# Softplus in a Mamba block: its three parts added by TensorE in PSUM in place of two VectorE additions

## The chip, the cores and the metric

The kernel runs on one core of one Trainium2 chip. The metric is the device time of one execution in microseconds (us). The engines are TensorE (PE, with its weight loads PEld), VectorE (DVE), ScalarE (ACT) and GpSimd (POOL); SyncE (SP) issues most of the DMAs.

## The reference

The program is a hybrid network of two layers on 32 sequences of 256 tokens with 128 features: a bidirectional Mamba block, a recurrence, two attention blocks and several mixtures of experts. Only the Mamba block is touched by the change. For each of two directions (the sequence as it is, and reversed) it computes:

```python
xz = x @ in_w.T;  xc, z = split(xz)                  # 256 inner features each
xc = silu(causal_conv(xc) + conv_b)
dt, Bm, Cm = split(xc @ xp_w.T)                      # 8, 16 and 16 columns
delta = softplus(dt @ dtp_w.T + dtp_b)
h = exp(delta * A) * h + (delta * u) * B             # 16 states per inner feature
y = sum(h * C) + xc * D
y = (y * silu(z)) @ out_w.T
```

The change is in how `softplus` is put together. The kernel has no softplus function to call; it uses softplus(v) = max(v, 0) + ln(1 + d) with d = exp(-|v|). Since 1 + d is rounded in 32 bits, it also adds what the rounding lost, d - ((1 + d) - 1). So delta is a sum of three parts: the logarithm, the correction, and max(v, 0).

## The kernel before

**Units.** `unit(k)` is a generator that does one direction of one chunk of 512 tokens (two sequences): a forward unit ("f") and then a backward unit ("b") for each of 16 chunks, 32 units in all. Features lie on the 128 partitions, the two halves of the 256 inner features side by side, so most tiles of the preparation are 128 x 1024 in 32-bit floats. `pipeline(unit, 16, 32)` (line 641) starts a new unit every 16 rounds and advances every active unit by one `yield` a round, the oldest first. A unit prepares for 24 rounds and then scans for 16, so that the preparation of one unit lies beside the scans of the unit before it.

**Preparation.** In the order of the text: the convolution as matmuls (lines 470 and 477), Silu (`act`, line 482), the projection to dt, B and C (488 and 490), written to DRAM (492). The softplus: a matmul gives v in PSUM (498), ScalarE computes `du` = max(v, 0) (499), |v| (500), `delta` = d (501), `one` = 1 + d (505) and `lg` = ln(one) (506). VectorE then makes the negated correction in place in `one` (508), subtracts it from `lg` (509), and adds `du` (510), which gives `delta`. GpSimd multiplies `delta` and `act` into `du` (511). Both go to DRAM (518) and come back in the layout of the scans (`load`, 545). The gate is a matmul of its own (521) and a Silu on ScalarE (530). ScalarE switches its function tables between Silu, Ln and Exp: each switch is an ACT_TABLE_LOAD of its own in the profile.

**Scans.** A unit has 8 groups of 4 scans. For each scan ScalarE computes `dA` (line 602, Exp, into one of three PSUM tiles), GpSimd `dBu` (606, four buffers), and VectorE scans (615). The products with C are made by VectorE (617 for two scans at once into `pr2`, two buffers; 625 for a third) and GpSimd (563, the fourth), and TensorE sums them over the states into `yps` (568) one group later.

**PSUM.** `pair()` gives the tile `m` of two banks, with one buffer: every matmul result of the preparation passes through this tile in turn, and the next one waits until the last reader of the one before is done.

**Order.** The engines execute their queues in order. The framework that records the kernel places the instructions into these queues by its own estimate of when each can start, so that the order on an engine is not just that of the text. `behind_scans()` ties a few VectorE instructions to the scan before them.

The lines that the change and the prediction speak of stand in this code:

Of the kernel before, what the change touches and what calls it, by code (L numbers as in the profile page):

```python
# [17 lines left out]
AF = mybir.ActivationFunctionType  # L18
ALU = mybir.AluOpType
# [3 lines left out]
P = 128  # L23
# [53 lines left out]
def halves(v):  # L77

    v = np.asarray(v)
    return np.moveaxis(v.reshape(2, P, *v.shape[1:]), 0, 1)  # L80


def col(v):
    return np.asarray(v).reshape(-1, 1)


def spaced(w, x):

    w = np.asarray(w)
    out = np.zeros((w.shape[0], 8, 16), np.float32)  # L90
    out[:, :, :HD] = w.reshape(w.shape[0], 2, 8, HD)[:, x]
    return out.reshape(w.shape[0], P)


def pack_inputs(i):
    mam, com, att, row, taps = (Packed() for _ in range(5))
    turn = np.arange(DI).reshape(2, 32, 4).transpose(0, 2, 1).reshape(DI)

    p = "L0_attn_a_"
    for s in "fb":  # L100

        w = i[p + "in_w_" + s]
        mam.add("in_w" + s, np.concatenate([w[:DI], w[DI:][turn]]).T)


        xp = i[p + "xp_w_" + s]
        turned = [xp[at : at + DS].reshape(4, 4, DI).transpose(1, 0, 2).reshape(DS, DI) for at in (DTR, DTR + DS)]
        mam.add("xp" + s, halves(np.concatenate([xp[:DTR], *turned, np.zeros((1, DI), np.float32)]).T))
        mam.add("out" + s, i[p + "out_w_" + s][:, turn])
        dtp = np.zeros((DTR + 2 * DS + 1, DI), np.float32)  # L110
        dtp[:DTR], dtp[-1] = i[p + "dtp_w_" + s].T, i[p + "dtp_b_" + s]
        mam.add("dtp" + s, dtp)
        mam.add("conv_b" + s, i[p + "conv_b_" + s].reshape(1, -1))

        a = np.asarray(i[p + "A_log_" + s]).reshape(2, 32, 4, 4, 4)
        mam.add("A_log" + s, a.transpose(1, 4, 0, 3, 2).reshape(P, 32))
        mam.add("D" + s, halves(i[p + "D_" + s]))
        taps.add(s, i[p + "conv_w_" + s][:, 0, :].T.reshape(1, -1))
    mam.add("one_row", np.eye(DTR + 2 * DS + 1, dtype=np.float32)[:, -1:])
    mam.add("turn", np.eye(P, dtype=np.float32)[:, turn[:P]])  # L120
    mam.add("proj", halves(i[p + "proj_w"].T))
    mam.add("proj_b", col(i[p + "proj_b"]))
    mam.add("g", col(i[p + "ln_gamma"]))
    mam.add("b", col(i[p + "ln_beta"]))

    p = "L0_ffn_"
    com.add("pw", i[p + "pw_w"].T)
    com.add("dw", i[p + "dw_kernel"][:, 0, :])
    com.add("dw_b", col(i[p + "dw_bias"]))
    com.add("pw_b", col(i[p + "pw_b"]))  # L130
    com.add("rt0", i[p + "router_w"].T)
    com.add("exp_w", i[p + "expert_w"].transpose(2, 0, 1))
    com.add("exp_b", i[p + "expert_b"].T)
    com.add("f0_out", i[p + "out_w"].T)
    com.add("f0_out_b", col(i[p + "out_b"]))
    com.add("norm_w", col(i[p + "norm_w"]))
    com.add("ffd", i[p + "ff_down_w"].T)
    com.add("ffd_b", col(i[p + "ff_down_b"]))
    com.add("ffu", i[p + "ff_up_w"].T)
    com.add("ffu_b", col(i[p + "ff_up_b"]))  # L140
    row.add("rt0_b", i[p + "router_b"].reshape(1, -1))

    p = "L0_attn_b_"
    for n in "ABC":
        com.add("rnn" + n, i[p + n].T)
    com.add("rnn_g", col(i[p + "gamma"]))
    com.add("rnn_b", col(i[p + "beta"]))

    p = "L1_attn_a_"
    for n, part in (("q", 0), ("k", 1)):  # L150
        w = i[p + "qkv_w"][:, part * P : (part + 1) * P]
        b = i[p + "qkv_b"][part * P : (part + 1) * P].reshape(1, P)
        for x in range(2):
            att.add(f"a{n}{x}", spaced(w, x))
            att.add(f"ab{n}{x}", spaced(b, x).T)
    att.add("wv", i[p + "qkv_w"][:, 2 * P :])
    row.add("bv", i[p + "qkv_b"][2 * P :].reshape(1, -1))
    att.add("rq", i[p + "rq_w"])
    att.add("rq_b", col(i[p + "rq_b"]))
    att.add("rkv", i[p + "rkv_w"])  # L160
    att.add("rk_b", col(i[p + "rkv_b"][:32]))
    row.add("rv_b", i[p + "rkv_b"][32:].reshape(1, -1))
    att.add("rout", i[p + "rout_w"])
    att.add("rout_b", col(i[p + "rout_b"]))
    att.add("aout", i[p + "out_w"])
    att.add("aout_b", col(i[p + "out_b"]))
    for n in ("gl", "gr"):

        g = np.zeros((H, HD, H, HD), np.float32)
        for h in range(H):  # L170
            g[h, :, h, :] = i[p + n + "_w"]
        att.add(n, g.reshape(P, P))

    p = "L1_attn_b_"
    swap = np.arange(P) ^ 1
    for n in ("Wq", "Wk"):
        for x in range(2):
            att.add(f"{n}{x}", spaced(i[p + n].T, x))
            att.add(f"{n}s{x}", spaced(i[p + n][swap].T, x))
    att.add("Wv", i[p + "Wv"].T)  # L180
    att.add("Wo", i[p + "Wo"].T)

    p = "L1_ffn_"
    att.add("f1_g", col(i[p + "ln_gamma"]))
    att.add("f1_b", col(i[p + "ln_beta"]))
    att.add("rt1", i[p + "router_w"])
    att.add("sgu", i[p + "shared_gate_up_w"])
    att.add("sdn", i[p + "shared_down_w"])
    gu = np.ascontiguousarray(i[p + "gate_up_w"])
    dn = np.ascontiguousarray(i[p + "down_w"].reshape(E, FF // P, P, P).transpose(0, 2, 1, 3))  # L190

    return mam, com, att, row, taps, gu, dn
# [81 lines left out]
def hybrid_kernel(ctx: ExitStack, tc, x_d, out_d, d, packs):  # L274
    nc = tc.nc
    mam, com, att, row, tap, cst, cst1 = (packs[k] for k in ("mam", "com", "att", "row", "tap", "cst", "cst1"))
# [13 lines left out]
    def K(name):  # L290
        return cst.view(cst_t, name) if name in cst.at else cst1.view(late_t["cst1"], name)
# [8 lines left out]
    ident = K("ident")  # L300
# [51 lines left out]
    with ExitStack() as ph:  # L352
# [4 lines left out]
        def M(name):  # L357
            return mam.view(mam_t, name)

        wconv, wout, A, skip = {}, {}, {}, {}  # L360
        with tc.tile_pool(name="mtap", bufs=1) as tp, tc.tile_pool(name="mprep", bufs=2, space=PSUM) as pp:
            tap_t = tp.tile([P, tap.n], F32, name="tap_t")
            nc.scalar.dma_start(tap_t, d["tap"].partition_broadcast(P))
            for k, s in enumerate("fb"):

                wconv[s] = wp.tile([P, DCONV, DI], F32, name="wconv" + s)
                at, _, w = tap.at[s]
# [45 lines left out]
        def unit(k):  # L413
# [3 lines left out]
            def pair():  # L417
                return ps.tile([P, 2, CH], F32, tag="m", name="m", bufs=1)

            def both(tag, bufs):  # L420
                return p2.tile([P, 2, CH], F32, tag=tag, name=tag, bufs=bufs)

            if s == "f":
                m = pair()
# [8 lines left out]
                m = pair()  # L433
# [11 lines left out]
                m = pair()  # L445
# [20 lines left out]
            m = pair()  # L466
            for h in range(2):
                for j in range(DCONV):
# [5 lines left out]
                        start=(j == 0),  # L474
                        stop=False,
# [10 lines left out]
            m = pair()  # L486
# [8 lines left out]
            delta, du = both("delta", 1), both("du", 1)  # L495
            m = pair()
# [5 lines left out]
            yield  # L502

            one, lg = both("sp", 1), both("lg", 1)
            nc.scalar.activation(one, delta, AF.Identity, bias=1.0)
            nc.scalar.activation(lg, one, AF.Ln)
            yield
            nc.vector.scalar_tensor_tensor(one, one, -1.0, delta, ALU.add, ALU.subtract)
            nc.vector.tensor_sub(lg, lg, one)
            nc.vector.tensor_add(delta, lg, du)  # L510
            nc.gpsimd.tensor_mul(du, delta, act)
            yield

# [5 lines left out]
            m = pair()  # L519
            for h in range(2):  # L520
# [4 lines left out]
                    start=True,  # L525
                    stop=True,
# [5 lines left out]
            for n, at in (("B", 0), ("C", DS)):  # L532
# [1 line left out]
                nc.sync.dma_start(  # L534
                    bc[n].rearrange("p g t -> p (g t)"), rows_of(xdbl_d, at, ((0, 32), (4, 4)), 4)
                )
            for _ in range(5):
                yield


# [93 lines left out]
            if s == "b":  # L634
                m = pair()
# [3 lines left out]
                yield  # L639

        pipeline(unit, 16, 2 * NCH)

    late = ctx.enter_context(tc.tile_pool(name="late", bufs=1))
# [15 lines left out]
    n = SPARE // 30  # L659
# [1050 lines left out]
```

## Time and profile before

| what | value |
|---|---|
| median of 3 runs | 6272.99 us (6271.46 to 6285.75) |
| the profiled execution | 6280.36 us, of which its span 6278.6 us |
| TensorE busy over the span | 5317.6 us (85%) |
| VectorE busy | 4184.9 us (67%) |
| ScalarE busy | 2664.6 us (42%) |
| GpSimd busy | 3335.2 us (53%) |
| end of the Mamba stage (last line 638) | 2104 us |

The profile shows one execution. Its slices divide the span into 40 equal parts of 157 us and give the busy tenths of each engine; the Mamba stage is slices 1 to 13 and part of 14. Queries of the trace give the busy times of a stretch, the waits of an engine ("A <- B" is A waiting for B), and the instructions in order of time: start in us, duration in us, engine, line, operation, output <- inputs, shapes, and in brackets the idle time before it and what ended it. A matmul of 32-bit floats appears as two records.

### The profile page before, as it was taken

The page shows a single profiled execution, that of the slowest core. Times are in us where ns is not written, and L with a number is a line of the kernel's source. Part 1 is how long each engine was busy: PE and PEld are TensorE (multiplying, and loading weights), DVE is VectorE, ACT ScalarE, POOL GpSimd, SP SyncE. Part 2 cuts the span into 40 slices and gives each one's busy share as a digit, 9 for nine tenths or more (in the row PEclk, how much of TensorE's full clock was granted, in tenths as well). Part 3 has the DMA queues.
Part 4 walks back from the last instruction along what each step waited for, and adds up shares of the span by engine and source line. Part 5 has one row for each costly group of instructions (what it writes and reads, how often), then busy time and mean ns, then how long its engine had stood idle before and what let it go on. Part 6 is the DMA issues. An engine that isn't in the chain of part 4 may idle for free. (4 is left out here: it accounts for less than half of the span.)

```text
span 6278.6 us, 73286 instructions
## 1 busy us (share of the span) xinstructions
PE 5317.6 (85%) x25538; PEld 2731.4 (44%) x25538; DVE 4184.9 (67%) x7070; ACT 2664.6 (42%) x4376; POOL 3335.2 (53%) x3074
## 2 busy tenths in 40 slices
PE   6777777777776799999989889897998999998897
PEld 2111111111111366865534444445884444444786
DVE  5999999999999664044645555554665666664565
ACT  4565555556565355334524434432221333333221
POOL 5888888888888565034634444443332333333332
PEclk8887888888888899588989999998998999997998
DMA  3232233322332660000000000003550000000555
GB/s 153 115 122 115 108 129 121 116 108 112 119 122 114 235 257 1 1 1 1 1 1 8 9 10 8 8 11 104 188 188 22 18 18 18 18 11 11 188 187 187
DMA packets 190417, 512.08 MB, mean 82 GB/s; under 512 B 22176, under 2 KB 75168, under 8 KB 164960
## 3 DMA queue, kind: packets, MB, share of 16 engines
q1 hardware_dynamic: 172192, 468.00, 20.7%
q0 software_dynamic: 17280, 35.69, 1.7%
q8 instruction: 202, 3.31, 0.2%
q10 hardware_dynamic: 576, 3.71, 0.2%
q14 instruction: 167, 1.37, 0.1%
HBM read 359.93 MB, written 147.38 MB: 81 GB/s over the span
## 5 line engine op out<-in xcount | busy, mean ns | idle before, releaser
L606 POOL TENSOR_TENSOR dBu<-widedu,bcB 128x512 f32<-128x512 f32 x1024 | 1334.0, 1324 | 250.7 <-DVE h L615 132.8
L615 DVE TENSOR_TENSOR_SCAN h<-dA,dBu 128x512 f32<-128x512 f32 x768 | 941.3, 1226 | 108.7 <-ACT dA L602 37.8
L568 PE MATMUL yps<-pr,cst_t 128*32 128x512 f32 x2048 | 702.5, 719 | 300.0 <-POOL pr L563 129.4
L930 POOL TENSOR_SCALAR_AFFINE_SELECT e<-e 128x2048 f32<-128x2048 f32 (+1 forms) x256 | 343.1, 1352 | 600.7 <-ACT e L1041 388.5
L1406 POOL DMA_INDIRECT rows_out<-y,goes x284 | 271.8, 957 | 558.5 <-DVE y L1404 451.5
L602 ACT ACTIVATE dA<-widedelta,Af 128x510 f32<-128x510 f32 x512 | 351.3, 689 | 398.4 <-DVE h L615 311.0
L994 DVE TENSOR_REDUCE nm<-st 128x2 f32<-128x512 f32 x512 | 324.3, 684 | 267.6 <-PE st L990 266.7
L602 ACT ACTIVATE dA<-widedelta,Ab 128x510 f32<-128x510 f32 x512 | 346.9, 687 | 354.5 <-DVE h L615 237.1
L568 PEld LDWEIGHTS yps<-pr,cst_t 128*32 128x32 f32 x2048 | 98.8, 120 | 870.2 <-POOL pr L563 308.1
L1181 ACT ACTIVATE s<-s 128x512 f32<-128x512 f32 x284 | 179.0, 630 | 575.9 <-DVE s L1180 329.2
L314 POOL TENSOR_TENSOR rstd<-var,cst_t 128x4 f32<-128x4 f32 x128 | 130.0, 1016 | 514.0 <-DVE var L312 512.1
L775 POOL TENSOR_TENSOR comb<-comb,ye 128x512 f32<-128x512 f32 x224 | 284.7, 1275 | 181.2 <-DVE ye L774 74.8
L1054 ACT ACTIVATE e<-st 128x512 f32<-128x512 f32 x512 | 271.6, 599 | 178.0 <-PE st L1050 146.0
L563 POOL TENSOR_TENSOR pr<-hs,bcC 128x512 f32<-128x512 f32 x256 | 339.8, 1328 | 13.3 <-DVE hs L615 13.0
L615 DVE TENSOR_TENSOR_SCAN hs<-dA,dBu 128x512 f32<-128x512 f32 x256 | 308.9, 1207 | 16.5 <-ACT dA L602 16.5
L1295 POOL DMA_INDIRECT rows_in<-xt,slot x256 | 254.0, 992 | 119.5 <-issue 99.1
L617 DVE TENSOR_TENSOR pr<-h,bcC 128x1024 f32<-128x1024 f32 x256 | 309.9, 1210 | 7.8
L1182 DVE TENSOR_TENSOR hh<-s,u_ps 128x512 f32<-128x512 f32 x284 | 195.3, 688 | 169.8 <-ACT s L1181 165.5
L1387 PE MATMUL g_ps<-xb,gu 128*128 128x256 f32 x1136 | 302.1, 389 | 3.6 <-ACT xb L1370 2.3
L1396 PE MATMUL yps<-dn,hh 128*128 128x128 f32 x2272 | 290.6, 276 | 5.3 <-DVE hh L1182 5.3
L1387 PE MATMUL u_ps<-xb,gu 128*128 128x256 f32 x1136 | 293.4, 381 | 0.0
L1396 PEld LDWEIGHTS yps<-dn,hh 128*128 128x128 f32 x2272 | 282.4, 192 | 14.0 <-DVE hh L1182 6.8
(348 smaller groups left out, 11021.0 us busy)
## 6 DMA issues: line engine op xcount, KB each, us to landing
gu<-in_gu SPq DMA_DIRECT2D x142, 512.0 KB, 3.7
rows_in<-zero SPq DMA_DIRECT2D x60, 1170.0 KB, 18.7
widedelta<-delta_d SPq DMA_DIRECT2D x64, 1024.0 KB, 6.8
widedu<-du_d SPq DMA_DIRECT2D x64, 1024.0 KB, 5.1
dn<-in_dn SPq DMA_DIRECT2D x142, 256.0 KB, 3.9
bcB<-xdbl_d SPq DMA_DIRECT2D x32, 1024.0 KB, 5.3
bcC<-xdbl_d SPq DMA_DIRECT2D x32, 1024.0 KB, 7.2
xr<-rows_in SPq DMA_DIRECT2D x142, 130.0 KB, 3.9
```

The costliest lines, as they stand in the source:

```text
L563: nc.gpsimd.tensor_mul(pr, hs, bc["C"][:, g, :])
L568: nc.tensor.matmul(yps[32 * k : 32 * k + 32, :], K("states"), pr, start=False, stop=(g == 3), skip_group_check=True, tile_position=(0, 32 ...
L602: nc.scalar.activation(two(dA)[:, :, 1:L], two(steps)[:, :, 1:L], AF.Exp, scale=A[s][:, at : at + 1])
L606: nc.gpsimd.tensor_mul(dBu, duw[:, k, :], bc["B"][:, g, :])
L615: scan[0] = nc.vector.tensor_tensor_scan(*views, 0.0, ALU.mult, ALU.add)
L617: nc.vector.tensor_mul(pr2, h2, bc["C"][:, g, :].unsqueeze(1).to_broadcast([P, 2, CH]))
L775: nc.gpsimd.tensor_add(comb, comb, ye)
L930: nc.gpsimd.affine_select(e, e, [[0, n], [sign, P]], ALU.is_gt, 0.0, base=base, channel_multiplier=-sign)
L994: nc.vector.tensor_reduce(n1[:, x, 2 * r : 2 * r + 2], o.rearrange("p (j k) -> p j k", j=2), AX.X, ALU.max, negate=True,)
L1387: nc.tensor.matmul(o[:, j, :], gu[:, at : at + P], xb, start=True, stop=True)
L1396: nc.tensor.matmul(yps[:, t, :], hh[:, k, t * P : (t + 1) * P], dn[:, k, :], start=(k == 0), stop=(k == FF // P - 1),)
L1406: i = nc.gpsimd.indirect_dma_start(rows_out[:, :], bass.IndirectOffsetOnAxis(ap=goes[:, t : t + 1], axis=0), y[:, t, :], None)
```

## The change

In the changed kernel `one` holds -(1 + d) (the bias comes from a new column `minus` of -1 in the packed weights), and Ln takes it with scale -1. One VectorE instruction makes the correction with its own sign. Then six matmuls through the identity (three inputs for each of the two halves) add `lg`, `one` and `du` in a tile `m` in PSUM, and ScalarE copies the sum into `delta`. GpSimd's product follows as before. The softplus has one round more; one round of the later waiting is taken out, so that the loads and the scans stay in the same rounds. Lines of the changed kernel after the softplus are six higher than before (509, the VectorE instruction; 515, the matmuls; 516, the copy; 517, the product).

```diff
+    mam.add("minus", np.full((P, 1), -1.0))
...
             one, lg = both("sp", 1), both("lg", 1)
-            nc.scalar.activation(one, delta, AF.Identity, bias=1.0)
-            nc.scalar.activation(lg, one, AF.Ln)
-            yield
-            nc.vector.scalar_tensor_tensor(one, one, -1.0, delta, ALU.add, ALU.subtract)
-            nc.vector.tensor_sub(lg, lg, one)
-            nc.vector.tensor_add(delta, lg, du)
+            nc.scalar.activation(one, delta, AF.Identity, bias=M("minus"), scale=-1.0)
+            nc.scalar.activation(lg, one, AF.Ln, scale=-1.0)
+            yield
+            nc.vector.scalar_tensor_tensor(one, one, 1.0, delta, ALU.add, ALU.add)
+            yield
+
+            m = pair()
+            for h in range(2):
+                for n, t in enumerate((lg, one, du)):
+                    nc.tensor.matmul(m[:, h, :], ident, t[:, h, :], start=(n == 0), stop=(n == 2))
+            nc.scalar.copy(delta, m)
             nc.gpsimd.tensor_mul(du, delta, act)
             yield
...
-            for _ in range(5):
+            for _ in range(4):
                 yield
```

## The prediction

> **What bounds the kernel now.** I read the slices of the span first, then the busy time of the Mamba stage alone, then who waits for whom in it, then the queues instruction by instruction around two softplus blocks. (The chain that ended last covers only the expert layers at the end, and no line of this change.) Row of the slices, and busy times of a stretch of 30 whole units (columns: length, PE, PEld, DVE, ACT, POOL, granted clock, DMA share, GB/s):
>
> ```profile
> DVE  5999999999999664044645555554665666664565
> ...
> 100.00:2050.00 1950.00, 1390.28 (x3435) 357.32 (x3434) 1793.24 (x1704) 1128.21 (x1432) 1702.03 (x1291) 0.83 0.30 117
> ```
>
> The Mamba stage ends at 2104 us with line 638. In it VectorE is busy in 92% of the time and GpSimd in 87%, TensorE in 71%, ScalarE in 58%. What VectorE waits for in the same stretch:
>
> ```profile
> DVE h L615 <- ACT dA L602: 37.8, 45, 2.7
> DVE sp L508 <- ACT lg L506: 23.1, 15, 1.6
> DVE hs L615 <- ACT dA L602: 16.5, 15, 1.4
> ```
>
> That is 77.4 us, all on ScalarE (columns: us in total, times, longest); TensorE and GpSimd are not in the list, and GpSimd's own waits are on VectorE. So VectorE sets the stage; its instructions otherwise start back to back. The order of both kernels as built, put side by side, is the same on every engine after the Mamba stage, and all tiles lie at the same addresses. So the whole effect lies in those 2104 us.
>
> Now the two softplus blocks of one pair of units. First on VectorE, the forward unit's (from 923 us) and the backward unit's (from 980 us):
>
> ```profile
> 923.27 1.39 DVE L508 SCALAR_TENSOR_TENSOR sp<-sp,delta 128x1024 f32<-128x1024 f32 x1 [1.56 <-ACT lg L506]
> 925.33 1.23 DVE L615 TENSOR_TENSOR_SCAN h<-dA,dBu 128x512 f32<-128x512 f32 x1 [0.66 <-ACT dA L602]
> 926.47 1.21 DVE L509 TENSOR_TENSOR lg<-lg,sp 128x1024 f32<-128x1024 f32 x1
> 927.59 1.22 DVE L615 TENSOR_TENSOR_SCAN h<-dA,dBu 128x512 f32<-128x512 f32 x1
> 928.72 1.21 DVE L510 TENSOR_TENSOR delta<-lg,du 128x1024 f32<-128x1024 f32 x1
> 929.84 1.21 DVE L617 TENSOR_TENSOR pr<-h,bcC 128x1024 f32<-128x1024 f32 x1
> ...
> 980.27 1.68 DVE L509 TENSOR_TENSOR lg<-lg,sp 128x1024 f32<-128x1024 f32 x1
> 981.88 1.22 DVE L615 TENSOR_TENSOR_SCAN h<-dA,dBu 128x512 f32<-128x512 f32 x1
> 983.02 1.20 DVE L510 TENSOR_TENSOR delta<-lg,du 128x1024 f32<-128x1024 f32 x1
> 984.14 1.21 DVE L615 TENSOR_TENSOR_SCAN h<-dA,dBu 128x512 f32<-128x512 f32 x1
> ```
>
> An operation costs VectorE the distance to the next start, not its duration. ScalarE at the first of these blocks:
>
> ```profile
> 917.49 1.05 ACT L505 ACTIVATE sp<-delta 128x1024 f32<-128x1024 f32 x1
> 918.55 1.28 ACT L530 ACT_TABLE_LOAD   x1
> 919.85 1.02 ACT L530 ACTIVATE gate<-m 128x1024 f32<-128x1024 f32 x1
> 920.89 1.28 ACT L506 ACT_TABLE_LOAD   x1
> 922.18 1.06 ACT L506 ACTIVATE lg<-sp 128x1024 f32<-128x1024 f32 x1
> 923.26 1.28 ACT L602 ACT_TABLE_LOAD   x1
> 924.55 2.73 ACT L602 ACTIVATE dA<-widedelta,Ab 128x510 f32<-128x510 f32 x4
> ```
>
> In the forward unit the gate's Silu stands ahead of Ln, so VectorE waits 1.56 us for Ln and 0.66 us for the next dA.
>
> **Removed from VectorE.** Lines 509 and 510. Forward unit: 927.59 - 926.47 = 1.12 and 929.84 - 928.72 = 1.12. Backward: 1.61 and 1.12. A pair of units: 4.97 us. Unit 0 has no scans beside it and is counted below; the other 31 units are 15.5 pairs: **77 us** off the engine that sets the stage. The kept line 508 has the same two inputs and I leave its price.
>
> **Added on TensorE.** Six matmuls through the identity a unit. The nearest row has the same shape and type:
>
> ```profile
> 973.60 1.99 PE L521 MATMUL m<-xpad,mam_t 128*128 128x512 f32 x4 [0.82 <-DVE x L638]
> ```
>
> Two matmuls (four records) take 1.99 us, so six take 6.0; over 30 units 179, and TensorE rises from 1390 us to some 1570 of about 1865 (84%). I cost this at nothing. What covers it: products of a group of four scans reach TensorE a group later, and prod2 has two buffers, prod four (two a group), so VectorE needs a group's buffers back only two groups on. A group lasts 7.0 us (L615 starts at 862.79 and 869.80). The convolution already puts 10.1 us of matmuls in that queue (925.48 to 935.57), and no wait of VectorE on TensorE follows. The six split: one waits for Ln alone, five (5.0 us) for line 509 of the new kernel. Queued behind them are one group's L568 products (lines 574 now). Cover gone, the price is up to 6.0 us a unit.
>
> **Added and moved on ScalarE.** A copy of 128x1024 out of PSUM a unit. Row: line 499, the same shape out of PSUM, 1.02 us. As built, the gate now follows the copy in every unit, since both use the one PSUM pair m; so it no longer shares a table switch with Ln in the forward units. Exp reloads rise from 78 to 94: 16 x 1.28 = 21 us. ScalarE grows by 53 us to some 1180 of 1865 (63%). What counts is whether dA comes late.
>
> Gain: in the forward unit Ln starts 2.3 us earlier (gate and its table gone from ahead of it) less one dA moved in front of it (0.69). Walked on from 917.49: dA to 919.2, table, Ln to 921.6, table, next dA at 923.5. VectorE, free at 921.7, does one scan to 922.9, line 509 to 924.2, the next scan at once. The 1.56 and the 0.66 are gone: 2.2 us a pair.
>
> Loss: copy, two dA, then table, Silu, table: 3.6 us without a dA, 4.3 until the next is ready. Three dA tiles let ScalarE run three scans ahead, at 7.0/4 = 1.75 us a scan 5.2 us of cover, 3.6 where the three have no product between them. In the forward unit the five matmuls end at 929.2, the copy's turn comes at 929.8, and the dA after the gate is ready at 937.1, scan needed at 937.7: no wait. In the backward unit POOL's product releases TensorE at about 981.7, the sum is there at 986.7, two microseconds after the copy's turn, and the dA after the gate is about 0.9 us late. I take 1.0 us a pair; bounds 0 and 5.6 (2.8 in each unit: copy 1.0 plus 4.3 less a cover of 3.6, plus a wait of 1.1 for the sum). The rest of the 77.4 I leave as it is. Net over 15 pairs: (2.2 - 1.0) x 15 = **18 us gained**; between 51 lost and, if every wait went, 77 gained.
>
> The Trainium skill speaks against the extra switches: "ScalarE: Activation LUTs", section "What ACT_TABLE_LOAD costs", gives 1283 ns and a drain of about 1380 ns for every switch. Here the load starts 0.01 us after the operation before it ends, and Silu 0.02 after the load: no drain shows, 1.28 is the price. By the page 16 switches would take 43 us of ScalarE and the gate's stretch 6.4 us, past the cover by about 1.9: 16 x 1.9 = 30 us lost, and a gain of 63 in place of 93. I take the row.
>
> **Moved on GpSimd and the queues.** The product du (line 517, 2.35 us) waits for the copy; queued behind it are dBu products, for which scans wait. It now stands after dBu 17 and 53 of a pair's 64, before after 13 and 50, that is 3 to 4 scans later, when the copy is done by the walk above. dBu has four buffers and a group costs GpSimd 5 x 1.27 = 6.4 us against VectorE's 7.0, so it stays ahead: 1702 of 1865 is 91%. It is even relieved: two dBu beside lines 509 and 510 took 4.41 us at 926.64, else 2.5. Cost nothing; cover gone, up to 2.4 us a unit. SP's writes of delta and du and the gate's step go 5 to 7 us later, B and C keep their order; the scans that read them begin 11 to 15 scans (19 to 26 us) after du, and write plus load need 3.1 + 6.8. Hidden. The conv of the next unit waits for the gate and act moves four scans, with the same slack behind it. One more column in mam_t: nothing.
>
> **Start.** Unit 0 has no cover: Ln would end at 56.3, line 509 at 57.6, five matmuls at up to 1.2 us to 63.5, copy 64.5, against 62.5 now for delta: **2 us lost**.
>
> **Sum.** 77 + 18 - 2 = 93. The profiled execution took 6280.4 us (span 6278.6) and should be near 6187; the median of the runs shown is 6273.0: 6273 - 93 = **6180 us**.
>
> **Rivals.**
> - *ScalarE's waits go too.* Shorter gaps without dA in every unit, 40 to 60 us more: 6130. For it: 77 us of waits are all there. Against: xdbl's wait for TensorE (2.0 us at 910.5) is untouched. 0.12.
> - *dA becomes late.* The gate's stretch after the copy shows in each unit with 1.5 to 2 us: 77 + 33 - 31 x 1.8 - 2 = 52, with the drain of the page or GpSimd late about 25 to 30 gained: 6225 to 6245. For it: the covers differ from the needs by under a microsecond. 0.13.
> - *VectorE was not the limit, GpSimd is:* 87% busy, a stall at du eats the gain; 6260 to 6285. Against: it waits 221 us for scans in dBu alone. 0.05.
> - *Slower: TensorE's burst reaches VectorE.* Five matmuls in an in-order queue hold up the products, and line 617 of the old kernel (623) waits for its buffer. It decides from 2.5 us a unit on; if all 6.0 surfaced, 31 x (6.0 - 2.5) = 109: 6380. Against: the 10.1 us burst shows nothing. 0.10.
>
> **How the numbers follow.** The main case has 0.60. 0.3% of 6273, about what a measurement can tell, is 19 us. Faster: 0.60 + 0.12 + 0.13 = 0.85; same 0.05; slower 0.10. The range holds the main case and most of the first two rivals: 6135 to 6240.
>
> **What would show it.** Right: the pair's period, now 126.2 us (line 638, 210.8 to 2104.0 in 15 steps), falls to about 120; the wait of sp for lg is gone; no wait of VectorE on TensorE; exp reloads 94 at 1.28 us. Wrong: VectorE waiting for dA by more than 110 us, for prod2 on TensorE, or for dBu on GpSimd; or any difference after the Mamba stage.

## The result

The changed kernel takes 6237.7 us (median of 7 runs, 6234.4 to 6256.5), the kernel before 6275.4 beside it: the ratio is 0.9945, 95% interval 0.9931 to 0.9958. It is faster by 0.55%, some 35 us, where 93 were forecast. A repeat on another chip gave 0.9946 (0.9931 to 0.9961).

All of it lies in the Mamba stage. In the two profiled executions its last line, 638 before and 644 now, starts at 2058.6 us in place of 2104.0, 45.4 us earlier, and the span shrank by 45.9 (6278.6 to 6232.7). That is some 10 us more than the ratio says: each profile shows a single execution. Two views of the changed kernel: line 644 (times: shortest, median, longest in ns; first and last start), and the busy times of the stretch that was shown of before (PE, PEld, DVE, ACT, POOL, clock, DMA, GB/s).

```profile
L644 DVE SCALAR_TENSOR_TENSOR x<-m,mam_t,x x16: 724/726/752, 212.0 to 2058.6; 128x512 f32<-128x512 f32 x16
```

```profile
100.00:2050.00 1950.00, 1467.19 (x3877) 422.07 (x3876) 1776.10 (x1684) 1194.49 (x1512) 1700.39 (x1323) 0.88 0.31 117
```

A pair of units now takes (2058.6 - 212.0) / 15 = 123.1 us, before 126.2: 3.1 us less, where 6.2 were forecast. The two stretches say how it splits. VectorE was busy 1793.2 of 1950 us, which is 116.1 us of a pair, and is now 1776.1, or 112.1: 4.0 us less work, where 5.0 were forecast. Its idle time rose from 10.1 to 11.0 us a pair. The forecast had that fall by 1.2.

What VectorE waits for now, in the same stretch (us in total, times, longest):

```profile
DVE hs L621 <- ACT dA L608: 47.3, 14, 4.5
DVE h L621 <- ACT dA L608: 30.4, 36, 2.2
DVE h L621 <- POOL dBu L612: 6.6, 11, 0.6
...
DVE pr L623 <- PE yps L574: 0.5, 1, 0.5
```

The wait for Ln, 23.1 us before, is not in the list. A new one is: 47.3 us in 14 waits, one to a pair, of 3.4 us on average. Here is one of them, on VectorE, ScalarE, TensorE and GpSimd in turn:

```profile
975.32 1.23 DVE L623 TENSOR_TENSOR pr<-h,bcC 128x1024 f32<-128x1024 f32 x1
980.99 1.22 DVE L621 TENSOR_TENSOR_SCAN hs<-dA,dBu 128x512 f32<-128x512 f32 x1 [4.44 <-ACT dA L608]
```

```profile
969.58 1.28 ACT L536 ACT_TABLE_LOAD   x1
970.87 1.02 ACT L536 ACTIVATE gate<-m 128x1024 f32<-128x1024 f32 x1
971.91 1.28 ACT L608 ACT_TABLE_LOAD   x1
973.21 0.69 ACT L608 ACTIVATE dA<-widedelta,Af 128x510 f32<-128x510 f32 x1
979.22 0.60 ACT L428 ACTIVATE sq<-m 128x512 f32<-128x512 f32 x1 [5.33 <-PE m L426]
979.72 0.58 ACT L430 COPY xc<-m 128x512 f32<-128x512 f32 x1
980.18 1.31 ACT L608 ACTIVATE dA<-widedelta,Af 128x510 f32<-128x510 f32 x2
```

```profile
972.07 1.04 PE L574 MATMUL yps<-pr,cst_t 128*32 128x512 f32 x2 [1.01 <-DVE pr L631]
975.26 1.92 PE L574 MATMUL yps<-pr,cst_t 128*32 128x512 f32 x2 [2.15 <-POOL pr L569]
977.11 2.08 PE L426 MATMUL m<-x,cst_t 128*128 128x512 f32 x2
```

```profile
967.96 2.37 POOL L517 TENSOR_TENSOR du<-delta,act 128x1024 f32<-128x1024 f32 x1
970.27 3.72 POOL L612 TENSOR_TENSOR dBu<-widedu,bcB 128x512 f32<-128x512 f32 x3
973.95 1.26 POOL L569 TENSOR_TENSOR pr<-hs,bcC 128x512 f32<-128x512 f32 x1
```

Read from the bottom. GpSimd's product pr comes at 973.95, behind du and three dBu. TensorE's L574 waits 2.15 us for it, and behind L574 in the queue stands L426, the first matmul of the next chunk's layer norm: the gate has released the tile m at 971.89, but L426 starts only at 977.11. ScalarE's Square (L428) waits 5.33 us for that matmul, and the two dA behind it in ScalarE's queue do not start before it is done, at 980.18. The Square stands one dA behind the gate's two table switches, so ScalarE comes to it with no further dA in hand, and VectorE waits 4.44 us. ScalarE's waits at the Square in the stretch, before and now:

```profile
ACT sq L427 <- PE m L425: 12.9, 14, 1.0
ACT sq L428 <- PE m L426: 59.6, 14, 5.3
```

### The profile page after: what moved, and what is told of

Its sections match the earlier page's. It is cut to its first block, busy times and chain, and to the rows that moved or that the text cites. A ratio compares the mean times of both kernels' runs of the same rounds, so it can differ in the third digit from the quotient of the medians.

```text
span 6232.7 us, 73938 instructions
## 1 busy us (share of the span) xinstructions
PE 5356.8 (86%) x25850; PEld 2792.6 (45%) x25922; DVE 4117.2 (66%) x7006; ACT 2710.2 (43%) x4424; POOL 3289.4 (53%) x3074
## 5 line engine op out<-in xcount | busy, mean ns | idle before, releaser
L612 POOL TENSOR_TENSOR dBu<-widedu,bcB 128x512 f32<-128x512 f32 x1024 | 1294.8, 1284 | 249.9 <-DVE h L621 162.0
L574 PE MATMUL yps<-pr,cst_t 128*32 128x512 f32 x2048 | 579.9, 645 | 244.8 <-POOL pr L569 102.7
L574 PEld LDWEIGHTS yps<-pr,cst_t 128*32 128x32 f32 x2048 | 86.8, 112 | 704.8 <-POOL pr L569 228.0
L621 DVE TENSOR_TENSOR_SCAN hs<-dA,dBu 128x512 f32<-128x512 f32 x256 | 308.3, 1204 | 48.8 <-ACT dA L608 47.3
```

The costliest lines, as they stand in the source:

```text
L574: nc.tensor.matmul(yps[32 * k : 32 * k + 32, :], K("states"), pr, start=False, stop=(g == 3), skip_group_check=True, tile_position=(0, 32 ...
L612: nc.gpsimd.tensor_mul(dBu, duw[:, k, :], bc["B"][:, g, :])
L621: scan[0] = nc.vector.tensor_tensor_scan(*views, 0.0, ALU.mult, ALU.add)
```

## The experiments

The theory from here on (A): the missing gain is in ScalarE's wait at the Square, which the gate, now behind the sum, has come to stand right in front of. The rivals (B) differ by run. The Mamba stage is read from the line that adds to x: its last start is the end of the stage, and last less first start over 15 is the period of a pair (126.2 us before, 123.1 in the change). The runs were made on several chips; a ratio is always to the kernel before on the same chip. The kernel before was profiled on one chip only. What lies behind the stage took 4172 to 4182 us in the profiles of one chip and 4202 to 4253 in those of two others, so ratio and end of the stage need not move together.

**The gate back ahead of the sum.**

```diff
-            one, lg = both("sp", 1), both("lg", 1)
...
             m = pair()
             for h in range(2):
...
-            yield
             gate = both("gate", 2)
             nc.scalar.activation(gate, m, AF.Silu)
+
+            one, lg = both("sp", 1), both("lg", 1)
...
```

The whole block of the softplus sum, with the writes of delta and du, moves behind the gate.

> The changed kernel with one edit: the gate's two matmuls and its Silu are put back ahead of the softplus sum (in the round of 1+d and Ln), where the tile m is free. Theory A (the lost gain is ScalarE's wait for the layer norm's first matmul, which the late gate pushes right behind the gate's table switches): the single wait of 3 to 5 us a pair for dA goes, Ln and Silu partly share a switch again, and the Mamba stage ends near 2058.6 - 16 x 3 = about 2010 to 2025 us, the kernel at 6190 to 6205. Rival B (the six matmuls in TensorE's queue, or the copy, cost VectorE the missing 50 us): the end of the stage stays at 2050 to 2065, the kernel at 6230 to 6245.

Measured: ratio 0.9999 (0.9987 to 1.0011), stage end 2087.3. Neither theory had that. The wait at the Square did go (1.6 us are left of it), but others came:

```profile
DVE h L622 <- ACT dA L609: 101.2, 107, 2.6
DVE sp L521 <- ACT lg L519: 21.8, 31, 1.1
```

Ln is late again, now in every unit, and waits for dA rose to 101 us; ScalarE waits for the matmul of xdbl in both units of a pair (81.5 us, in the change 33.1). So the whole kernel gains nothing measurable with the gate ahead of the sum. The stage does gain something: the pair's period is 124.0 us, 2.2 less than before. Half of these 34 us go at the start, where the first line that adds to x comes at 227.7 us in place of 210.8, and the other half does not show in the time of the whole kernel; why is not shown.

**The Square one dA later.**

```diff
                 nc.tensor.matmul(m[:, 0, :], K("center"), x, start=True, stop=True)
+                yield
                 sq = p2.tile([P, CH], F32, tag="ln_sq", name="sq", bufs=1)
...
                 nc.gpsimd.tensor_tensor(rstd, var, K("mhalf"), ALU.pow)
                 yield
-                yield
```

> The changed kernel with one edit: the Square and the copy that read the layer norm's first matmul are recorded one round later (a later empty round is taken out), which puts exactly one dA more in front of them on ScalarE and nothing else. Theory A: VectorE has one scan more to do during ScalarE's wait, so the wait of hs for dA falls from 4.4 to about 2.8 us a pair: the stage ends at 2058.6 - 16 x 1.6 = about 2033, the kernel near 6212. Rival B: no change, 2058 and 6238.

Measured: ratio 0.9904 (0.9886 to 0.9923), stage end 2024.3. That is theory A, with 34 us for the 26 that it named, although from one chip to another; the pair's period falls from 123.1 to 120.7. ScalarE still waits 62.1 us at the Square, but VectorE has one scan more to do meanwhile. At the same place of a pair:

```profile
967.72 2.59 DVE L621 TENSOR_TENSOR_SCAN h<-dA,dBu 128x512 f32<-128x512 f32 x2 [1.48 <-ACT dA L608]
```

It waits 1.48 us in place of 4.44. Run again on another chip:

> Again the changed kernel with the Square one dA later, beside the others on one chip: 0.989 to 0.992 of the kernel before, the stage ending 25 to 40 us before that of the kernel with the gate late alone.

0.9884 (0.9866 to 0.9902), a little better than expected, and stage end 2025.0, which is 31 us before the kernel with the gate late alone (2055.8, next), as expected.

**The gate late, the additions left on VectorE.**

```diff
             nc.vector.scalar_tensor_tensor(one, one, -1.0, delta, ALU.add, ALU.subtract)
+            yield
             nc.vector.tensor_sub(lg, lg, one)
...
-            for _ in range(5):
+            for _ in range(4):
```

> The kernel before with one edit: an empty round after the first of the three VectorE operations, so that the sums and the gate come one round later, as in the change; the additions stay on VectorE. It shows what the moved gate does without TensorE's sum. Theory A: the waits for Ln go (2.2 us a pair), exp reloads rise to 93, and part of them comes back as ScalarE's wait for the layer norm's matmul (1 to 4 us a pair): the stage ends between 2085 and 2120, the kernel between 6255 and 6290. Rival B (the gate's place is of no account): 2104 and 6275.

Measured: ratio 0.9926 (0.9897 to 0.9956), stage end 2055.4, and again on another chip:

> Again the kernel before with the gate one round later and the additions on VectorE, now beside the others on one chip. Both theories: 0.990 to 0.996 of the kernel before; as fast as the change within 0.3%.

0.9925 (0.9909 to 0.9940), stage end 2055.8. Both theories of the first run were wrong: this kernel, in which nothing is moved to TensorE, is as fast as the change (0.9945), if not a little faster. The gate stands behind Ln here too (93 reloads of Exp in place of 78), so the wait for Ln is gone. Of VectorE's waits for ScalarE this is left, before 77.4:

```profile
DVE h L617 <- ACT dA L604: 28.7, 30, 2.6
```

The Square stands one dA behind the gate, as in the change, and does not wait at all. The difference is on TensorE: its matmul, L425 here, stands ahead of the products L570 and starts as soon as the gate has released the tile, at 956.48.

```profile
956.54 1.12 PE L425 MATMUL m<-x,cst_t 128*128 128x512 f32 x2 [0.89 <-ACT gate L532]
958.88 1.04 PE L570 MATMUL yps<-pr,cst_t 128*32 128x512 f32 x2 [1.22 <-DVE pr L627]
```

```profile
957.80 0.69 ACT L604 ACTIVATE dA<-widedelta,Af 128x510 f32<-128x510 f32 x1
958.43 0.58 ACT L427 ACTIVATE sq<-m 128x512 f32<-128x512 f32 x1
```

From the end of the gate to the start of this matmul it is 0.06 us in this kernel, 3.5 before, and 4.0 to 5.2 in the change, pair after pair. (Before, the matmul stood behind the products too, but two dA lay between the gate and the Square.) So theory A names half of the cause: in these kernels the Square right behind the gate costs VectorE time only where its matmul stands behind the products, the last of which waits for GpSimd. The framework's order put it there; no run changed that place alone.

**The sum twice.**

```diff
-                for n, t in enumerate((lg, one, du)):
-                    nc.tensor.matmul(m[:, h, :], ident, t[:, h, :], start=(n == 0), stop=(n == 2))
+                for n, t in enumerate((lg, one, du, lg, one, du)):
+                    nc.tensor.matmul(m[:, h, :], ident, t[:, h, :], start=(n in (0, 3)), stop=(n in (2, 5)))
```

> The changed kernel with the six matmuls of the sum done twice over (the second pass starts the sum anew, so the result is the same): 6 us more of TensorE a unit and nothing else. Theory A (TensorE's matmuls are covered): the stage grows by at most 1 us a unit, 0 to 32 us in all, mostly because the copy is waited for longer: the kernel at 6238 to 6270. Rival B (the burst holds up the products and so VectorE): 3 to 6 us a unit, 100 to 190 us in all, the kernel at 6335 to 6430.

Measured: ratio 0.9923 (0.9899 to 0.9947), stage end 2048.3. With six more matmuls a unit the stage even ends earlier than with the sum once, although its start is 17 us later (228.6 at the first line 644); the pair's period is 121.3. But the edit did not add matmuls and nothing else: the framework's order moved with the longer sum. The layer norm's matmul stands ahead of the product that waits for GpSimd, as with the gate late alone, and starts 0.46 us behind the gate; ScalarE's wait at the Square is gone, although the Square is still one dA behind the gate. VectorE's longest waits:

```profile
DVE h L621 <- ACT dA L608: 35.0, 32, 1.4
DVE hs L621 <- POOL dBu L612: 19.0, 30, 1.1
DVE var L440 <- PE m L437: 12.4, 15, 0.9
```

No product of VectorE waits for TensorE, and nothing like 3 to 6 us a unit is lost. Rival B is out; a small price of the matmuls can't be read from this run.

**The change itself, on the chip of the next three.**

> The changed kernel itself, beside the three below on one chip, so that they can be compared with it. Both theories: the Mamba stage ends within 5 us of 2058.6 and the ratio to the kernel before is 0.993 to 0.996.

0.9946 (0.9931 to 0.9961), stage end 2069.8, not within 5 us of 2058.6. So ends of the stage from different chips are not to be compared closer than some 12 us: the ends of this and of three other kernels that were run on two chips lie 0.4 to 12.1 us apart.

**No wait at the Square.** Square and copy read x, not the centred result; the centring is left out of the values.

```diff
-                nc.scalar.activation(sq, m[:, 0, :], AF.Square)
+                nc.scalar.activation(sq, x, AF.Square)
...
-                nc.scalar.copy(xc, m[:, 0, :])
+                nc.scalar.copy(xc, x)
```

> The changed kernel with the forward unit's Square and copy reading x itself, not the centred matmul's result (the centring is thereby left out of the values; the matmul is still executed): ScalarE no longer waits for TensorE at this place, and all else stays in its order. Theory A (this wait is what ate the gain): the wait of hs for dA, 47 us in the stage, goes, and the stage ends at 2005 to 2020. Rival B (the time comes up elsewhere, at the copy or at xdbl): 2035 or later.

Measured: ratio 0.9896 (0.9878 to 0.9915), stage end 2043.5, 26 us before the change on the same chip, with a period of 122.0 us for 123.6. The wait of hs for dA (50.9 us in the change there) is gone to nothing, and half of it came up at the next matmul of the same layer norm:

```profile
DVE h L621 <- ACT dA L608: 35.3, 45, 2.5
DVE var L440 <- PE m L437: 28.6, 15, 2.7
```

Between the theories: the wait at the Square is real and costs what it shows, but the product that holds TensorE's queue up there stands ahead of the layer norm's second matmul too, and so VectorE waits for that one.

**Square and xdbl later.**

```diff
+            yield
             xdbl = p2.tile([NX, CH], F32, tag="xdbl", name="xdbl")
...
-            for _ in range(4):
+            for _ in range(3):
```

> The kernel with the Square one dA later (2024.3 us at the end of the stage) and one more edit of the same kind: xdbl, for whose matmul ScalarE waits 2 to 3 us in each pair, is recorded one round after its matmul, and everything behind it one round later. Theory A (what is left of VectorE's waits are ScalarE's waits for TensorE): 1 to 2 us a pair less, the stage ends at 1995 to 2015. Rival B (the queue's order is made by the framework's own estimate, so xdbl stays where it was): 2020 to 2030.

Measured: 0.9873 (0.9855 to 0.9890), stage end 2019.3 on the chip where the change ended at 2069.8, just ahead of rival B's range. Again:

> Again the fastest kernel so far, beside the others on one chip: 0.986 to 0.989 of the kernel before.

0.9889 (0.9871 to 0.9907), stage end 2031.4, beside 0.9884 and 2025.0 for the Square alone. ScalarE's wait for the matmul of xdbl is 30.6 us in both. So the edit at xdbl adds nothing that was repeated. The Square later is what counts, and both kernels beat the change and the kernel before: 1.0 to 1.3% under the latter.

**All three parts and the correction on TensorE.** Ten matmuls a unit; VectorE has no softplus operation.

```diff
-            nc.vector.scalar_tensor_tensor(one, one, 1.0, delta, ALU.add, ALU.add)
-            yield
             m = pair()
             for h in range(2):
-                for n, t in enumerate((lg, one, du)):
-                    nc.tensor.matmul(m[:, h, :], ident, t[:, h, :], start=(n == 0), stop=(n == 2))
+                nc.tensor.matmul(m[:, h, :], ident, one[:, h, :], start=True, stop=False)
+                nc.tensor.matmul(m[:, h, :], ones[:, 0:P], ones, start=False, stop=False)
+                for n, t in enumerate((delta, lg, du)):
+                    nc.tensor.matmul(m[:, h, :], ident, t[:, h, :], start=False, stop=(n == 2))
+            yield
```

> The kernel with the Square one dA later, and the correction too is summed on TensorE: -(1+d), a one, d, the logarithm and max(v,0), ten matmuls a unit in place of six, and no VectorE operation of the softplus is left. Theory A (VectorE sets the stage, TensorE is covered): 31 x 1.6 us less, the stage ends near 1975 to 1990, the kernel 0.7 to 0.8% below the one with the Square later. Rival B (TensorE's queue becomes the limit with 4 more us a unit): no gain or a loss, 2024 or later.

Measured: 0.9924 (0.9910 to 0.9937), stage end 2043.6, 26 us before the change there but behind the kernel with Square and xdbl later (2019.3). VectorE has less to do and waits more, now for TensorE as well:

```profile
DVE h L621 <- ACT dA L608: 42.4, 62, 2.6
DVE hs L621 <- ACT dA L608: 24.0, 15, 1.6
DVE pr L623 <- PE yps L574: 23.0, 12, 2.2
```

That is rival B's outcome. This is the only kernel here in which the products' buffers were late; the sum twice had more matmuls and not this wait, which speaks for the place in the queue and not the amount of work. That was not taken apart further.

**The same reordering, the additions on VectorE.** The kernel with the gate late alone, and Square and xdbl later as above.

> The additions stay on VectorE; the gate one round later, the Square and xdbl one round later: the edits of the fastest kernel so far without the change itself. It shows what the sum on TensorE is worth where both kernels have the same reordering. Theory A (the two VectorE operations are worth their full start-to-start time, 77 us, where the waits are gone): 55 to 77 us more than the fastest kernel beside it, the stage ending 55 to 77 us later. Rival B (most of the change's gain was the gate's place): 10 to 35 us more.

Measured: 0.9936 (0.9920 to 0.9952), stage end 2058.9; the kernel beside it with the sum on TensorE 0.9889 and 2031.4. That is rival B: with the same rounds the sum on TensorE is worth 27.5 us. With the better kernel of each kind on this chip (2055.8 with the gate late alone, 2025.0 with the sum on TensorE and the Square later) it is worth 31 us. In both comparisons some 77 us of VectorE's operations are gone. The second pair of kernels shows where the rest is, in the stretch from 100 to 2000 us: VectorE is busy 1791.4 of 1900 us with the additions, 116.1 us of a pair of 123.15, and 1758.7, or 111.8 of 120.8, without: 4.3 us less. Idle are 7.0 and 9.0: 2.0 of the 4.3 come back as waits.

## Why the prediction was right or wrong

The sign, the stage, and the engine that sets it were right, but the gain was 35 us for 93. The time lies just inside the range because that was drawn to hold most of the first two rivals; the main case did not come true. In the profiles 3.1 us a pair are missing: 1.0 of them because VectorE's work fell less than forecast, 2.1 because its idle time rose by 0.9 and did not fall by 1.2. (VectorE did not start back to back outside its listed waits, as the prediction has it: 78 of its 157 idle microseconds in the stretch were in gaps that the list does not name, and 84 of 174 are now. They bear little on the difference.)

*Removed from VectorE: right in kind, a little too large.* 4.97 us a pair were forecast, 4.0 is how much the busy time fell. The kept operation was left at its price and took longer: on average 1655 ns (line 509) for 1402 (line 508), 0.5 us a pair. It now mostly starts when a GpSimd instruction beside it has 0.6 us left, where it was 0.3 before (last section). The other 0.5 us of the difference is not assigned.

*Added on TensorE at nothing: right as far as it went.* VectorE's products hardly wait for TensorE (0.5 us in all), and twice the matmuls did not change that. But the walk asked only after the products; what another matmul in TensorE's queue makes ScalarE wait was not asked, and there the loss is.

*The forward unit's wait for Ln: right.* It was to go, and went: after the walked order VectorE does a scan, line 509 and a scan without a gap.

```profile
904.87 1.23 DVE L621 TENSOR_TENSOR_SCAN h<-dA,dBu 128x512 f32<-128x512 f32 x1
906.01 1.68 DVE L509 SCALAR_TENSOR_TENSOR sp<-sp,delta 128x1024 f32<-128x1024 f32 x1
907.62 1.22 DVE L621 TENSOR_TENSOR_SCAN h<-dA,dBu 128x512 f32<-128x512 f32 x1
```

But it needed only the gate's place, not the sum: the kernel with the gate late alone shows it, and gains as much as the whole change. The prediction booked the removal of the operations and of the wait as one change's gain and did not ask what the order alone would bring.

*The failed step: the loss on ScalarE in the backward unit.* "The dA after the gate is about 0.9 us late. I take 1.0 us a pair." The walk ended at the first dA behind the gate. At that dA little is lost: it is done at 973.90, and its scan starts at 973.98, after 0.61 us in which GpSimd's dBu came last. The walk should have gone on to the next instruction in ScalarE's queue, the Square, and from there to TensorE's queue, where its matmul stands behind a product that GpSimd makes only after du and three dBu. Measured: 3.4 us a wait, 47.3 us in all, or 3.0 us a pair for the 1.0 expected. The runs show it from three sides: one dA more ahead of the Square takes 2.4 us off a pair's period, without the wait 1.6 us go, and in the two kernels above whose matmul stands ahead of that product there is no wait. Why the framework put it behind the product in the change stays open. The bound of 5.6 us a pair had room for the loss; the chosen value had not.

*The table switches: the row was right.* 94 reloads of Exp, as counted, at 1283 ns each, with 1.6 us of idle time before all of them together: no drain shows. The estimate with the drain that the Trainium skill states ("ScalarE: Activation LUTs", section "What ACT_TABLE_LOAD costs"), a gain of 63, lies nearer to the outcome than the sum by the row (93), but by luck: what is missing is mostly the wait at the Square.

*GpSimd and the start: nearly right.* VectorE waits 6.6 us in all for dBu, where nothing was forecast; the first line that adds to x comes 1.2 us later, for 2 forecast. After the Mamba stage nothing moved.

The rival that comes nearest is "dA becomes late", at 25 to 55 us gained. Its price came from one place in a pair, not from every unit.

## What to carry to other kernels

Where an engine is taken off the path by moving work behind another result, follow the queue of the engine that takes over past the moved instruction, to the next one that waits for somebody: the moved stretch uses up the work in hand, and the next wait then shows. Look too where the producer of what it waits for stands in its own queue: the same Square, one dA behind the same gate, waited 5.33 us in the change and not at all in two kernels whose matmul stood ahead of the products. Before a change is credited with its gain, make the kernel that has only its reordering: here one empty round gave as much as the change. And an operation taken off the busiest engine is worth less than its duration once the others are close behind: here some 2.3 us of 4.3.

## What was not expected of the hardware

How long a VectorE operation with both inputs in SBUF takes depends on where it starts within a GpSimd instruction. Line 509 of the changed kernel took 1199 to 2264 ns, median 1687, line 508 before 1225 to 1744, median 1390, for the same shape and two inputs. The longest of them:

```profile
1082.74 1.27 POOL L569 TENSOR_TENSOR pr<-hs,bcC 128x512 f32<-128x512 f32 x1
1082.83 2.26 DVE L509 SCALAR_TENSOR_TENSOR sp<-sp,delta 128x1024 f32<-128x1024 f32 x1
```

GpSimd's product has 1.18 us left when line 509 starts, and line 509 takes these and 1.08 us more. The working holds for each of the 37 cases in both kernels whose GpSimd instruction stands as a record of its own: with 0.3 us left line 508 takes 1.39, with 0.6 left line 509 takes 1.68, with 1.01 left 2.09, always 1.07 to 1.09 us more than what is left. It holds the other way too: two dBu that started just behind the old line 509 took 4.41 us at 926.64, for 2.5 elsewhere. So in these records the later of the two does not advance until the earlier is done. Line 623, with one input in PSUM, kept its time (1192 to 1226 ns, before 1196 to 1226).

The stage ended 11 us apart in two profiles of one kernel on different chips (2058.6 and 2069.8).
